# A message-passing layer whose scatter feeds nine epochs: the first group prepared alone, and the last filters made early

## The chip, the core and the metric

The kernel runs on one core of a Trainium2 chip. Its engines work side by side, each on its own list of instructions, in order, and wait for each other by semaphores: PE (TensorE, matmuls; PEld are its weight loads), DVE (VectorE), ACT (ScalarE), POOL (GpSimd) and SP (SyncE, which here only issues DMAs). The metric is the device time of one execution in microseconds (us), median of ten.

## What is computed

`x` has 12500 rows of 128; there are 400000 edges, sorted by `dst`, with `src` at random.

```python
h = jnp.maximum(_layernorm(x, axis=-1), 0.0)
h = h @ W_in2f.T                                           # then, with edge_attr as f_ij:
Wij = smu(f_ij @ W_f1.T + b_f1) @ W_f2.T + b_f2
Wij = Wij * edge_weight[:, None]
x_ij = h[dst] * Wij
agg = segment_sum(x_ij, src, num_segments=12500)
out = x + smu(agg @ W_o1.T + b_o1) @ W_o2.T + b_o2
```

Of every edge, a row of `h` (at `dst`) is multiplied by a filter `Wij`, made from its 20 attributes by two matmuls with a bent line (`smu`, an erf gate, done by a Gelu and a linear term) between them, and the product is summed into the row `src`.

## The kernel before

**Tiles.** An edge tile is 128 edges; 4 tiles are a *group* (512 edges, `GRP`), 8 tiles a *supertile* (`SUP`). There are 3125 tiles, 782 groups, 391 supertiles. The targets are cut in 98 *bins* of 128 rows.

**Epochs.** The supertiles are dealt to nine epochs (`PARTS`: 59, 59, 59, 59, 48, 37, 27, 27, 16). In its epoch, each tile's 128 messages go by one indirect DMA from POOL (`send`, L599) into a DRAM buffer of that epoch, `buf`, sorted by bin of `src`: each row to a slot that was counted for it. During the next epoch the buffer is read back (`fetch`, L630), and each bin is summed into `agg` by matmuls with a 0/1 matrix (`choose`, `se`, L641; `add`, `pg`, L654). One `add` matrix product of 128 rows is here called a *part*; an epoch has 98 bins times 6 parts (epochs 0 to 3), then 5, 4, 3, 3, 2. The last epoch's buffer is summed after the loop, with the two output matmuls interleaved.

**One pass of the loop** (`for g in range(NG)`) works on several groups at once, and its order is the program order of PE, DVE, ACT and SP, written by hand (`manual_schedule`); POOL and the DMAs follow by their waits:
- `turn(g)`, `send(g)`: PE transposes the messages (`pt`, L586), ACT copies them with the edge weight into `ms` (L596), POOL scatters (L599); `ms` has six buffers.
- `number(g+1)`, `weigh(g+1)` (second filter matmul, `pw`, L566), `gather(g+1)` (rows of `h` by a one-hot matmul on a window of 128 rows, `ph`, L547), `take(g+1)` (ACT copy, `hg`, L555), half of the parts of this pass, `mix(g+1)` (DVE product of filter and row, `mt`, L576).
- `hide(g+2)` (first filter matmul, `pu`, L516), `bend(g+2)` (Gelu, `ge`, L524), `count(g+2)` (`pc`, L464 and L465) and `read(g+2)` (four ACT reads, `jk`, L494), `smooth(g+2)` (DVE, `sm`, L532, reads `pu` and `ge`), `bins(g+3)`, the other half of the parts.
- three calls of `step()`, which in epoch 0 take the setup work off a list: the indices of the other tiles, the statistics and `h` of the other bins (24 units), the loads of `x`.

The parts of an epoch are spread evenly over its groups from the fifth on (`WAIT` = 4). PSUM has one bank each for `pu`, `pw`, `ph`, `pt`, `pc` (pool `ps1`, one buffer) and two for `pg`.

**The opening** (L682 to L722) loads the indices of 512 tiles, makes relative positions of `dst` (through a DRAM row `rel_dram` that is read back to all partitions, `rbc`), statistics and rows of `h` for the first four bins (`HEAD`), stores them in `h_dram` as three bfloat16 parts, reads windows of it back (`hw`), and takes groups 0 and 1 through the stages by hand. The stretch after the last scatter ("the end") is the last epoch's sum and the output.

The lines that set the parts' spread are

```python
lo = len(work) * (i - WAIT) // (ng - WAIT)
hi = len(work) * (i + 1 - WAIT) // (ng - WAIT)
```

Of the kernel before, what the change touches and what calls it, by code (L numbers as in the profile page):

```python
# [19 lines left out]
P = 128  # L20
# [14 lines left out]
BIG = 32768.0  # L35
ZP = 128


@with_exitstack
def gnn_kernel(  # L40
# [59 lines left out]
    bufs = [dram.tile([NB * CAP[k], ROW], F32, name=f"buf{k}") for k in range(EPOCHS)]  # L100
    tab = dram.tile([N + P, D], F32, name="tab")


# [157 lines left out]
    with tc.tile_pool(name="ld", bufs=4) as ld, \  # L261
# [13 lines left out]

        def fill(i):
            nc.vector.memset(fbufs[i], 1.0)

# [8 lines left out]
        def head_of(c):  # L287
# [5 lines left out]
            di, si, rel = rw[:, 0:n].bitcast(I32), rw[:, CH:CH + n].bitcast(I32), rw[:, 2 * CH:2 * CH + n]  # L293
            if c:
                rb = parts_tile()[:, :, 0, :]
            else:
                rb = edge.tile([P, SUP * P], BF, name="oh", bufs=3)[:, :CH].rearrange("p (j e) -> p j e", e=P)
            base_f = edge.tile([1, CH // SUP], F32, name="base_f")
# [7 lines left out]
            def based():  # L306
                nc.vector.tensor_copy(base_i[:, s0:s0 + m], di[0:1, 0:n:SUP])
                nc.vector.tensor_copy(base_f[:, :m], base_i[:, s0:s0 + m])
                nc.vector.tensor_copy(rel, di)

# [36 lines left out]
            def binned():  # L347
                nc.vector.tensor_scalar(di, si, 7, None, op0=ALU.arith_shift_right)
                nc.vector.tensor_copy(hi_b[:, a:a + n], di)

            def placed():
                nc.vector.tensor_scalar(di, si, P - 1, None, op0=ALU.bitwise_and)
                nc.vector.tensor_copy(lo_b[:, a:a + n], di)

            return dict(fetched=fetched, based=based, spread=spread, lowered=lowered, turned=turned, written=written,
                        limits=limits, bounded=bounded, binned=binned, placed=placed)


        one = head_of(0)
        one["fetched"]()  # L360
        nc.scalar.dma_start(x_sb[:, 0:HEAD, :], bin_rows(x, 0, HEAD))
        nc.scalar.dma_start(w_in, w_in_t)
        nc.vector.memset(w_f1, 0.0)
        nc.scalar.dma_start(w_f1[0:R, :], w_f1_t)
        nc.scalar.dma_start(w_f1[R:R + 1, :], b_f1)
        nc.scalar.dma_start(w_f2, w_f2_t)
        nc.scalar.dma_start(b2, b_f2.rearrange("o p -> p o"))
        nc.scalar.dma_start(w_sb[:, 0:CH], w_col[:, 0:CH])
        zr = edge.tile([P, 3 * D], BF, name="zr", bufs=1)
        nc.vector.memset(zr, 0.0)  # L370
        nc.scalar.dma_start(h_dram[NB * P:N + WIN, :], zr[:N + WIN - NB * P, :])
        for i in range(NF):
            fill(i)
        nc.vector.memset(zero, 0.0)
        clear(0, len(cleans) - 1, nc.scalar)
        spare = const.tile([P, 1], F32, name="spare")
        nc.scalar.activation(spare, eps, AF.Sqrt)

        def late_loads():

            nc.vector.memset(x_sb[:, NB - 1, :], 0.0)
            nc.vector.memset(w_sb[:, CH:CH + 1], 0.0)
            nc.gpsimd.dma_start(w_sb[:, CH:NT], w_col[:, CH:NT])
            nc.gpsimd.dma_start(w_o1, w_o1_t)
            nc.gpsimd.dma_start(w_o2, w_o2_t)
            nc.gpsimd.dma_start(b1, b_o1.rearrange("o p -> p o"))
            nc.gpsimd.dma_start(b2row, b_f2)
            nc.gpsimd.dma_start(bo2, b_o2.to_broadcast([P, P]))

# [7 lines left out]
        def load(s):  # L397
            if s >= NS:
                return
            t0, nt = sups[s]  # L400
            e0, n = t0 * P, nt * P
            fb = fbufs[s % NF]
            if s > 2:
                nc.sync.dma_start(fb[0:R, :n], f_t[:, e0:e0 + n])
            rb = ld.tile([P, SUP * P], BF, name="rbc")
            nc.sync.dma_start(rb[:, :n], rel_dram[:, e0:e0 + n].to_broadcast([P, n]))
            loaded[s] = (fb, rb)
            if s > 2:
                window(s)
# [18 lines left out]
        begins = {}  # L428

        def bins(g):  # L430

# [8 lines left out]
            if g in first:  # L440
                k = first[g]
                nc.vector.memset(co[:, 0], 0.0)
                m = sum(groups[i][1] for i in range(g, min(g + eps_of[k][1] * PER, NG)))
                begins[k] = (t, cnt.tile([P, max(n for _, n in eps_of) * SUP], F32, name="hic", bufs=2))
                nc.vector.tensor_scalar(begins[k][1][:, :m], hi_b[:, t:t + m], float(CAP[k]), None, op0=ALU.mult)
            else:
                pl, cl, nl = last.pop(0)
                nc.vector.tensor_add(co[:, 0], cl[:, nl - 1], pl[:, nl - 1])
# [60 lines left out]
        def hide(g):  # L509

            if g >= NG:
                return
# [6 lines left out]
        def bend(g):  # L519
            if g >= NG:  # L520
                return
            n = groups[g][1] * P
            ge = edge.tile([P, GRP * P], F32, name="ge")
            nc.scalar.activation(ge[:, :n], units_of[g][:, :n], AF.Gelu, scale=ZS)  # L524
            hidden[g] = ge

        def smooth(g):
            if g >= NG:
                return
# [20 lines left out]
        def take(g):  # L550
            if g >= NG:
                return
# [7 lines left out]
        def weigh(g):  # L560

            if g >= NG:
                return
            n = groups[g][1] * P
            pw = ps1.tile([P, GRP * P], F32, name="pw")
            nc.tensor.matmul(pw[:, :n], w_f2, hidden.pop(g)[:, :n], start=True, stop=True)  # L566
            pws[g] = pw

        mixed = {}

        def mix(g):
            if g >= NG:
                return
            n = groups[g][1] * P
            mt = edge.tile([P, GRP * P], F32, name="mt")
            nc.vector.scalar_tensor_tensor(mt[:, :n], pws.pop(g)[:, :n], b2, rows_of.pop(g)[:, :n],  # L576
                                           op0=ALU.add, op1=ALU.mult)
# [103 lines left out]
        WAIT = 4  # L681
        for s in range(3):  # L682
            nc.sync.dma_start(fbufs[s][0:R, :], f_t[:, s * SUP * P:(s + 1) * SUP * P])
        one["based"]()
        one["spread"]()
        one["bounded"]()
        one["lowered"]()
        one["turned"]()
        one["written"]()
        for s in range(3):  # L690
            load(s)
        nc.vector.tensor_scalar(w_f2, w_f2, GC, None, op0=ALU.mult)
        for b in range(HEAD):
            stats(edge, b)
        deviations(0, HEAD)
        rw = rowp.tile([P, ROWS, ROW], F32, name="rw")
        for step in rows_of_h(0, HEAD, *[rw[:, j * GRP:(j + 1) * GRP, 0:P] for j in range(3)], parts_tile(), bank):
            step()
        for s in range(3):
            window(s)  # L700
        late_loads()
        one["binned"]()
        bins(0)
        hide(0)
        bend(0)
        smooth(0)
        hide(1)
        bend(1)
        weigh(0)
        count(0)  # L710
        read(0)
        one["placed"]()
        pick(0)
        gather(0)
        number(0)
        take(0)
        mix(0)
        turn(0)
        send(0)
        smooth(1)  # L720
        bins(1)
        count(1)  # L722
        read(1)
        pick(1)
        bins(2)
        cleared = at_first = done = 0
        work = []
# [34 lines left out]
        single = [lambda b=b: stats(edge, b) for b in range(HEAD, NB)]  # L762
        steps = [one["limits"], loads.pop(0)]
        for c in range(1, NC):
# [4 lines left out]
            for f in mine:  # L769
                steps.append(f)  # L770
                if c > 1:
                    steps.append(single.pop(0))
        steps += loads
        for i in range(0, len(single), 2):
# [3 lines left out]
        for i in range(0, len(units_of_rows), 2):  # L778
            for pair in zip(*units_of_rows[i:i + 2]):
                steps += pair  # L780
        steps.append(output_bias)
        COUNT = len(steps)
        taken_steps = slot = 0

        def step():

            nonlocal taken_steps, slot
            slot += 1
            while taken_steps < COUNT and taken_steps * 3 * (eps_of[0][1] * PER - 12) < slot * COUNT:
                steps[taken_steps]()  # L790
                taken_steps += 1

        for g in range(NG):
            s = g // PER
            k = epoch[s]
            g0, ng = eps_of[k][0] * PER, min(eps_of[k][1] * PER, NG - eps_of[k][0] * PER)
            i = g - g0
            if g % PER == 0:
                load(s + 3)
# [21 lines left out]
            if k and i >= WAIT:  # L821
                lo = len(work) * (i - WAIT) // (ng - WAIT)
                hi = len(work) * (i + 1 - WAIT) // (ng - WAIT)
            if g:
                turn(g)
                send(g)
            step()
            number(g + 1)
            weigh(g + 1)
# [6 lines left out]
            bend(g + 2)  # L836
            count(g + 2)
            read(g + 2)
            smooth(g + 2)
            if g % PER == 0:  # L840
                pick((g + 4) // PER)
            bins(g + 3)
            parts(k - 1, hi)
            step()
            assert k == 0 or taken_steps == COUNT
# [225 lines left out]
```

## Time and profile before

| | |
|---|---|
| median of 10 runs | 4132.07 us (4129.55 to 4133.11) |
| the profiled execution | 4131.43 us, its span 4129.6 |
| PE busy | 3701.4 us (90%) |
| DVE, ACT, POOL busy | 3200.9, 2821.6, 3045.7 us |
| scatters (L599) | 3125, 0.963 us each |
| DMA | 834.71 MB, 202 GB/s over the span |
| first scatter, last scatter (start) | 32.90, 4020.17 us |

How to read it: busy time of an engine says little here, since the stages have different limits; POOL's issue time between two scatters does not count as busy. The trace lists instructions in order of time (start, duration, engine, line, operation, output and inputs, count, and in brackets the idle time ahead with what ended it); groups of instructions over a stretch (busy time, mean ns of one); and busy time stretch by stretch, with the count of instructions in brackets, then the granted clock of PE, the DMA engines' busy share and GB/s.

### The profile page before, as it was taken

What the parts mean: (1) busy time and instruction counts of PE and PEld (TensorE: products, weight loads), DVE (VectorE), ACT (ScalarE), POOL (GpSimd) and SP (SyncE); (2) the same over time, 40 slices, a digit from 0 to 9 for tenths busy, and PEclk for the clock granted to TensorE, in tenths of its full rate; (3) what the DMA queues carried; (4) which work ended last, traced back from release to release, by engine and by line L of the source; (5) the groups of instructions that cost most, each with busy time, mean ns of one, the idle gap of its engine ahead of it and who ended that gap; (6) DMA issues with size and microseconds to landing.
All of it is one profiled execution on the core that took longest, in us unless ns stands there. A gap on an engine that the chain in (4) does not pass through costs nothing. (4 is left out here: it accounts for less than half of the span.)

```text
span 4129.6 us, 74682 instructions
## 1 busy us (share of the span) xinstructions
PE 3701.4 (90%) x18498; PEld 2303.1 (56%) x18794; DVE 3200.9 (78%) x8553; ACT 2821.6 (68%) x11054; POOL 3045.7 (74%) x3165
## 2 busy tenths in 40 slices
PE   6878887999988999979999979999899899999999
PEld 2334434655545655546655546666566566565567
DVE  7888866877767877768877768888688788788777
ACT  5778875776666776657766757777677667677651
POOL 5777777777777777777777777777777777777762
PEclk9999998999999999989999989999999999999999
DMA  7857665766647666646666647676688689777568
GB/s 206 227 165 204 187 173 183 215 206 192 199 143 223 200 204 200 203 154 204 210 200 203 193 156 215 211 211 206 182 231 233 177 258 255 211 224 225 176 183 237
DMA packets 520970, 834.71 MB, mean 202 GB/s; under 512 B 84575, under 2 KB 334916, under 8 KB 520400
## 3 DMA queue, kind: packets, MB, share of 16 engines
q1 hardware_dynamic: 405932, 614.18, 51.8%
q0 software_dynamic: 100304, 208.14, 15.6%
q10 hardware_dynamic: 14292, 7.53, 0.6%
q8 instruction: 152, 2.49, 0.3%
q14 instruction: 290, 2.38, 0.2%
HBM read 456.16 MB, written 373.36 MB: 201 GB/s over the span
## 5 line engine op out<-in xcount | busy, mean ns | idle before, releaser
L599 POOL DMA_INDIRECT buf<-ms,ix x3125 | 3009.9, 963 | 990.0 <-issue 257.9
L654 PEld LDWEIGHTS pg<-se,rw 128*128 128x128 f32 x8036 | 1088.1, 192 | 152.0 <-issue 13.6
L596 ACT ACTIVATE ms<-pt,w_sb 128x128 f32<-128x128 f32 x3125 | 904.0, 392 | 358.7 <-DMA buf<-ms,ix 156.3
L654 PE MATMUL pg<-se,rw 128*128 128x128 f32 x8036 | 1109.6, 276 | 7.6 <-DVE se L641 7.6
L494 ACT ACTIVATE jk<-pc,nbig 128x98 f32<-128x98 f32 x3125 | 1025.9, 352 | 3.3 <-PE pc L465 2.7
L566 PE MATMUL pw<-sm,w_f 128*128 128x512 f32 x1564 | 882.1, 646 | 46.5 <-DVE sm L532 41.9
L524 ACT ACTIVATE ge<-pu 128x512 f32<-128x512 f32 x782 | 469.2, 600 | 550.3 <-PE pu L516 526.8
L576 DVE SCALAR_TENSOR_TENSOR mt<-pw,b,hg 128x512 f32<-128x512 f32 x782 | 583.7, 746 | 325.4 <-ACT hg L555 323.9
L516 PE MATMUL pu<-f,w_f 128*128 128x512 f32 x1564 | 809.8, 600 | 4.2 <-DVE sm L532 4.2
L586 PE MATMUL pt<-ident,mt 128*128 128x128 f32 x3125 | 495.5, 282 | 319.2 <-DVE mt L576 316.2
L641 DVE TENSOR_TENSOR se<-irow_ps,rw 128x1536 f32<-128x1536 f32 (+1 forms) x345 | 587.8, 1704 | 151.6 <-DMA rw<-buf 130.6
L532 DVE SCALAR_TENSOR_TENSOR sm<-pu,ge 128x512 f32<-128x512 f32 x782 | 536.0, 685 | 197.2 <-ACT ge L524 187.6
L494 ACT ACTIVATION_READ_ACCUMULATOR jk<-pc,nbig 128x1 f32 x3125 | 680.0, 218 | 0.0
L555 ACT ACTIVATE hg<-ph 128x512 f32<-128x512 f32 x782 | 470.0, 601 | 284.4 <-PE ph L547 282.4
L547 PE MATMUL ph<-oh,hw 128*128 128x512 bf16 x2050 | 626.1, 384 | 16.8 <-DMA hw<-h_dram 1.2
L586 PEld LDWEIGHTS pt<-ident,mt 128*128 128x128 f32 x3125 | 351.7, 142 | 416.0 <-DVE mt L576 408.3
L451 DVE TENSOR_TENSOR co<-co,po 128x98 f16<-128x98 f16 x2353 | 501.9, 213 | 81.2
L547 PEld LDWEIGHTS <-hw 128*128 128x128 bf16 x2346 | 231.7, 99 | 551.7 <-issue 451.1
L437 DVE TENSOR_TENSOR po<-irow_ps,hi_b 128x392 f16<-128x392 f32 x782 | 434.7, 556 | 0.0
L566 PEld LDWEIGHTS pw<-sm,w_f 128*128 128x128 f32 x1564 | 237.1, 191 | 176.3 <-DVE sm L532 172.6
L516 PEld LDWEIGHTS pu<-f,w_f 128*128 128x128 f32 x1564 | 251.8, 195 | 27.8 <-DVE sm L532 5.8
L464 PE MATMUL pc<-co,ones_h 128*128 128x392 f16 x782 | 258.6, 331 | 1.2 <-ACT ms L596 1.2
(119 smaller groups left out, 1699.5 us busy)
## 6 DMA issues: line engine op xcount, KB each, us to landing
rw<-buf SPq DMA_DIRECT2D x292, 774.0 KB
rbc<-rel_dram SPq DMA_DIRECT2D x390, 256.0 KB
buf<-zero SPq DMA_DIRECT2D x243, 387.0 KB
buf<-ms,ix POOLq DMA_INDIRECT x3125
buf<-zero SPq DMA_DIRECT2D x193, 258.0 KB
hw<-h_dram SPq DMA_DIRECT2D x391, 96.0 KB
rw<-buf SPq DMA_DIRECT2D x49, 645.0 KB
f<-in_f_t SPq DMA_DIRECT2D x390, 80.0 KB
```

Source lines behind the costliest of these rows:

```text
L451: nc.vector.tensor_add(co[:, j], co[:, j - 1], po[:, j - 1])
L494: nc.scalar.activation(jk, pc[:, j], AF.Relu, bias=nbig, accum_out=sl[:, j:j + 1])
L516: nc.tensor.matmul(pu[:, :n], w_f1, loaded[g // PER][0][:, o:o + n], start=True, stop=True)
L532: nc.vector.scalar_tensor_tensor(sm[:, :n], units_of.pop(g)[:, :n], LIN, hidden[g][:, :n], op0=ALU.mult, op1=ALU.add)
L547: nc.tensor.matmul(ph[:, :n], hw[:, q * D:(q + 1) * D], oh[:, o:o + n], start=(q == 0), stop=(q == 2))
L566: nc.tensor.matmul(pw[:, :n], w_f2, hidden.pop(g)[:, :n], start=True, stop=True)
L576: nc.vector.scalar_tensor_tensor(mt[:, :n], pws.pop(g)[:, :n], b2, rows_of.pop(g)[:, :n], op0=ALU.add, op1=ALU.mult)
L586: nc.tensor.transpose(pt[:, j, :], mt[:, j * P:(j + 1) * P], ident)
L596: nc.scalar.activation(ms[:, j, 0:P], pt[:, j], AF.Copy, scale=w_sb[:, t + j:t + j + 1])
L599: i = nc.gpsimd.indirect_dma_start(out=bufs[k][:, :], out_offset=bass.IndirectOffsetOnAxis(ap=ix[:, j:j + 1], axis=0), in_=ms[:, j, :], in ...
L641: nc.vector.tensor_tensor(se[:, :m], irow_ps.unsqueeze(1).to_broadcast([P, m, P]), rows_in[c][:, :m, P:P + 1].to_broadcast([P, m, P]), op= ...
L654: nc.tensor.matmul(pgs[0][:, g, :], rows_in[c][:, o, 0:P], sel[c][:, o, :], start=(q == 0), stop=(q == Q[k] - 1))
```

## The change

Two things are changed.

**The opening.** The first bin and the first 24 tiles (`FEW`, three supertiles) are prepared alone: their own small index loads (`ds`, `ss`), one bin's statistics and `h`, which stays in SBUF (`h_first`) and serves as the window of supertiles 0 to 2. Group 0 gets its one-hot from PE transposes (`spread_group`, `pick_group`). The rest of the first 512 tiles' preparation and bins 1 to 3 become a list `opening`, two items at each `step()` of the first passes. Fills and some loads go to POOL, six weight loads from POOL to steps on SP.

**The filters.** The filters of the last 43 supertiles (all of epochs 7 and 8, 86 groups) are made early: from group 126 on, at every fifth pass, `ahead_hide`, and in the next pass `ahead_smooth`, `ahead_weigh` and `ahead_keep`, make one group's filter, which SP stores in DRAM (`filters`). In the last 86 groups `hide`, `bend`, `smooth`, `take` and `weigh` return at once; `load` brings the filter (512 KB per supertile) in place of the attributes, and `mix` reads it from SBUF and the rows straight from `ph`. In the passes with early work the parts are thinned by 2.5 and 2.5, and the other passes take them.

```diff
+AHEAD_OF = 43
+EVERY = 5
...
+    SOON = NS - AHEAD_OF
+    filters = [dram.tile([P, SUP * P], F32, name=f"filter{s}") for s in range(SOON, NS)]
...
         one = head_of(0)
+        ds = edge.tile([P, FEW], I32, name="ds", bufs=1)
...
+        h_first = const.tile([P, 1, 3, D], BF, name="h_first")
+        nc.sync.dma_start(ds, dst_col[:, 0:FEW])
+        nc.scalar.dma_start(x_sb[:, 0:1, :], bin_rows(x, 0, 1))
+        nc.sync.dma_start(ss, src_col[:, 0:FEW])
+        nc.scalar.dma_start(w_in, w_in_t)
+        fill(0, nc.vector)
+        nc.gpsimd.memset(w_f1, 0.0)
+        nc.gpsimd.dma_start(w_f1[0:R, :], w_f1_t)
...
+        fill(1, nc.gpsimd)
+        nc.gpsimd.memset(zero, 0.0)
+        clear(0, len(cleans) - 1, nc.gpsimd)
+        fill(2, nc.gpsimd)
...
@@ def load(s)
-            if s > 2:
+            if s >= SOON:
+                nc.sync.dma_start(fb[:, :n], filters[s - SOON][:, :n])
+            elif s > 0:
                 nc.sync.dma_start(fb[0:R, :n], f_t[:, e0:e0 + n])
...
@@ hide, bend, smooth, take, weigh
-            if g >= NG:
+            if g >= NG or g // PER >= SOON:
                 return
...
+        ahead = [g for g in range(NG) if g // PER >= SOON]
+        ahead_of = {}
+        for i, g in enumerate(ahead):
+            ahead_of[eps_of[0][1] * PER + 8 + i * EVERY] = g
...
+        def ahead_hide(g):
...
+            pu = ps1.tile([P, GRP * P], F32, name="pu")
+            nc.tensor.matmul(pu[:, :n], w_f1, fx[:, o:o + n], start=True, stop=True)
+            ge = edge.tile([P, GRP * P], F32, name="ge")
+            nc.scalar.activation(ge[:, :n], pu[:, :n], AF.Gelu, scale=ZS)
+            if g + 1 < NG and (g + 1) % PER == 0:
+                ahead_load(g + 1)
...
+        def ahead_smooth(g):
...
+            nc.vector.scalar_tensor_tensor(sm[:, :n], units_of.pop(g)[:, :n], LIN, hidden[g][:, :n],
+                                           op0=ALU.mult, op1=ALU.add)
...
+        def ahead_weigh(g):
...
+            pw = ps1.tile([P, GRP * P], F32, name="pw")
+            nc.tensor.matmul(pw[:, :n], w_f2, hidden.pop(g)[:, :n], start=True, stop=True)
...
+        def ahead_keep(g):
...
+            wx = edge.tile([P, GRP * P], F32, name="ge")
+            nc.scalar.activation(wx[:, :n], pws.pop(g)[:, :n], AF.Copy)
+            nc.sync.dma_start(filters[g // PER - SOON][:, o:o + n], wx[:, :n])
...
@@ def mix(g)
+            if g // PER >= SOON:
+                o = g % PER * GRP * P
+                pws[g] = loaded[g // PER][0][:, o:o + n]
...
@@ the opening, in order
+        nc.vector.tensor_copy(dsf, ds)
+        pb0 = spread_group(0)
...
+        stats(edge, 0)
+        few = edge.tile([FEW, P], BF, name="few", bufs=1)
+        nc.scalar.activation(few, pd[:FEW, 0:P], AF.Copy)
+        nc.sync.dma_start(rel_dram[0, 0:FEW * P].rearrange("(t e) -> t e", e=P), few)
+        few_bins()
+        deviations(0, 1)
...
+        normed()
+        turned()
...
+        pick_group(0, pb0)
+        shorn()
...
+        hide(0)
...
+        for b in range(1, HEAD):
+            stats(edge, b)
+        deviations(1, HEAD)
+        nc.scalar.activation(spare[:, 1:2], eps, AF.Gelu)
+        product()
+        bins(0)
...
+        first_part()
         bend(0)
+        other_parts()
         smooth(0)
+        pb1 = spread_group(1)
         count(0)
         read(0)
         gather(0)
         number(0)
         take(0)
+        weigh(0)
         mix(0)
...
         turn(0)
         send(0)
+        hide(1)
...
+        opening = [one["based"], heads[0], one["spread"], heads[1], one["lowered"], heads[2], one["turned"], heads[3],
+                   one["written"], heads[4], one["bounded"], heads[5], one["binned"], other_starts]
...
@@ the loop
-                lo = len(work) * (i - WAIT) // (ng - WAIT)
-                hi = len(work) * (i + 1 - WAIT) // (ng - WAIT)
+                load_of = [2.5 * (g0 + j in ahead_of) + 2.5 * (g0 + j - 1 in ahead_of) for j in range(WAIT, ng)]
+                even = (len(work) + sum(load_of)) / (ng - WAIT)
+
+                def upto_group(j):
+                    return len(work) if j == ng else min(len(work), max(0, round(even * (j - WAIT) - sum(load_of[:j - WAIT]))))
+                lo, hi = upto_group(i), upto_group(i + 1)
             if g:
                 turn(g)
                 send(g)
             step()
+            if g - 1 in ahead_of:
+                ahead_smooth(ahead_of[g - 1])
             number(g + 1)
             weigh(g + 1)
             gather(g + 1)
             take(g + 1)
             parts(k - 1, lo + (hi - lo) // 2)
             mix(g + 1)
             step()
             hide(g + 2)
             bend(g + 2)
             count(g + 2)
+            if g - 1 in ahead_of:
+                ahead_weigh(ahead_of[g - 1])
             read(g + 2)
+            if g - 1 in ahead_of:
+                ahead_keep(ahead_of[g - 1])
             smooth(g + 2)
             if g % PER == 0:
                 pick((g + 4) // PER)
             bins(g + 3)
             parts(k - 1, hi)
+            if g in ahead_of:
+                ahead_hide(ahead_of[g])
             step()
```

## The prediction

> **What bounds the kernel now.** I read the page first, then POOL's scatter line and the message copies that feed it over chosen stretches, then one group of the loop in order of time. The page:
>
> ```profile
> span 4129.6 us, 74682 instructions
> ...
> L599 POOL DMA_INDIRECT buf<-ms,ix x3125 | 3009.9, 963 | 990.0 <-issue 257.9
> ```
>
> Its first part gives POOL 74% of the span, PE 90%. POOL looks idle for a quarter, but its 3125 scatters are spaced by 0.96 us of work and about 0.30 us of issue. The second view, stretch by stretch, has L599 alone (stretch, length, busy, count):
>
> ```profile
> 700.00:860.00 160.00, 121.57 (x127) 1.00 0.68 208
> ...
> 2480.00:2880.00 400.00, 303.63 (x317) 1.00 0.71 213
> ...
> 3850.00:4000.00 150.00, 104.08 (x109) 0.97 0.70 211
> ```
>
> 127 scatters in 160 us is 1.26 us each, 5.05 us per group of four; nearly every stretch has that rate. Scatters start at 32.9, the last at 4020.2. So the span is 32.9 (opening) + 3124 x 1.263 = 3945.6 + 41.7 (lost between scatters) + 109.4 (the end after the last scatter). By the scatters' starts, epoch 0 loses 13.7 of the 41.7 (608.6 us for 471 intervals), epoch 8 loses 13.5 (170.1 for 124). **POOL sets the end, wherever the other engines supply a group in under 5.05 us.** How near they are, the same view of L596, the message copies (four per group), shows:
>
> ```profile
> 700.00:860.00 160.00, 39.29 (x136) 1.00 0.68 208
> ...
> 2480.00:2880.00 400.00, 93.59 (x324) 1.00 0.71 213
> ```
>
> In 700-860 the supply made 34 groups, 4.71 us each, and ran ahead of POOL; in epoch 4, 81 groups in 400 us, 4.94 each. Slack: 0.34 us per group in epochs 1 to 3, 0.11 in epoch 4. One group of that stretch, in order of time (start, duration):
>
> ```profile
> 786.51 1.03 PE L516 MATMUL pu<-f,w_f 128*128 128x512 f32 x2
> ...
> 787.37 0.33 PE L464 MATMUL pc<-co,ones_h 128*128 128x392 f16 x1
> ...
> 787.57 0.60 ACT L524 ACTIVATE ge<-pu 128x512 f32<-128x512 f32 x1 [0.71 <-PE pu L516]
> 787.70 0.83 PE L654 MATMUL pg<-se,rw 128*128 128x128 f32 x6
> ...
> 788.20 0.69 DVE L532 SCALAR_TENSOR_TENSOR sm<-pu,ge 128x512 f32<-128x512 f32 x1 [0.55 <-ACT ge L524]
> ...
> 788.37 0.60 PE L586 MATMUL pt<-ident,mt 128*128 128x128 f32 x4
> ```
>
> PE goes from step to step without a hole: from start to start `pu` takes 0.86, the counts 0.33, two matmuls of the add (one part) 0.22; in the lines ahead of these `pw` began at 784.46, the gather `ph` at 785.42, the next add at 786.07, so 0.96 and 0.65. PE sets the supply. And `sm`, which frees the only `pu` bank, ends at 788.89, after `pt` has begun.
>
> **The change, the opening.** Before, the first mix starts at 30.50 and the first scatter comes 2.4 us later:
>
> ```profile
> 30.50 0.75 DVE L576 SCALAR_TENSOR_TENSOR mt<-pw,b,hg 128x512 f32<-128x512 f32 x1 [1.10 <-ACT hg L555]
> ...
> 32.90 1.03 POOL L599 DMA_INDIRECT buf<-ms,ix  x1 [11.64 <-ACT ms L596]
> ```
>
> The new chain, by rows of before's first 33 us: indices land 2.0 us after issue at 0.75 (a store of `rel` issued at 12.61 frees its reload at 14.61), DVE is busy with a 0.91 fill until 3.2; five transposes to 4.8 (four took 1.16); ACT `few` and the first deviation to 5.4; reciprocal and normalising to 5.95; transpose and relu to 6.8; PE's `pu` (1.92) and the product to 8.5. ACT meanwhile waits for three more bins' statistics (8.1), a deviation, the Gelu table (1.28) and a dummy, to 9.9; two casts, a Gelu (0.60) and two DVE subtractions to 11.4; gather 1.5, copy 0.6, `pw`, to 14.6; mix to 15.4; first scatter 1.6 later, 17.0. POOL's new work there (fills of 0.91 to 1.6 each by the DVE fill and POOL's own 0.20 for an eighth; five DMAs of 0.6; clears) is over by 13. Gain 15.9. Then group 1: PE has a spread, three transposes and the adjoining steps ahead of its `turn`, where the second group trails by 9.7 us already now (32.90 to 42.63); I take 3 us off and bound the gain by 8 and 18. **-13.**
>
> The rows price these matmuls at a half-speed rate (1.92 for `pu`, 1.03 later) although the granted clock reads 0.97. The Trainium skill ("TensorE: Matmul & The Clock Gate", section "Part 1: The HAM clock gate") says that the array runs at half clock until about 3.4 us of sustained activity. By it `pw` and the gather would be warm already and the first scatter come near 15.4, an estimate; before's rows show 1.9 us pairs as late as 34 us, and I go by those.
>
> Six weight loads move from POOL to SP (0.4 us of issue each, in steps of epoch 0 that nobody awaits soon): nothing.
>
> **The end.** The last 86 groups lose `pu`, `pw`, Gelu, copy and `sm`: 1.82 us of PE, 1.2 of ACT, 0.69 of DVE each. In epoch 8 PE needs 5.4 to 5.6 per group; 3.7 is below POOL's 5.05, so its 13.5 go, and some 1.9 of epoch 7's. The reads grow from 80 to 512 KB per 10.1 us, 44 GB/s more on stretches with 219 to 226 and a busy share of 0.74 to 0.79; they are issued three supertiles (30 us) ahead, and the 774 KB fetches of rows land within 6 us. Should the queues fill up, late rows cost 0 to 6. **-15.** The 109 us after the last scatter are untouched.
>
> **The same work, early.** 86 groups move to groups 126 to 551, one in five: 22, 24, 24 items in epochs 1 to 3, 16 in epoch 4. The parts of the add are only shifted (5 fewer in the item's two groups, more elsewhere). An item costs PE 0.86 + 0.96 = 1.82, plus its waits:
> - `ahead_hide` needs the bank `pu`, which `smooth(g+2)` has just been given to read. PE arrives 0.86 + 0.33 + 2 x 0.22 = 1.64 after `pu`'s start; `sm` ends 2.38 after it (786.51 to 788.89). Wait 0.75. Behind it on PE stands everything else, first the `turn` of the next messages, for which ACT and POOL wait.
> - `ahead_keep` stands on ACT behind four reads (788.07 to 789.33, 2.82 after `pu`) and ends at 3.42; the next `pw` wants its bank at 0.86 + 0.33 + 0.96 + 0.44 + 0.58 = 3.17. Wait 0.25 to 0.3; the next message copies, behind the copy on ACT, need `turn` and come later anyway.
> - 25 of the 86 items have a choice (`se`, 1.75 on DVE) beside `ahead_smooth`: 0.3 to 0.8 each, 0.15 on average.
>
> Together 3.0 us. Against that, PE idles a little today (4.3 us before `pt` over the 34 groups, 0.63 per five); as fewer late mixes are met I take 0.5 back. **An item costs 2.5 of supply, the slack of five groups is 1.7.** So 0.8 x 70 = 56, less the lead that each epoch starts with (POOL's lag is 4 to 8 us there and 2 to 3 where it starves: 5 + 2 + 2): 47. Epoch 4: 16 x (2.5 - 0.55) - 2 = 29. **+76.** Bounds per item: 1.2 (no wait, all idle time refilled) to 3.3 (nothing absorbed, more collisions). The store of each filter (256 KB per 25 us, 10 GB/s) waits on SP for ACT; behind it are fetches of rows issued four tiles ahead, and the load of the next early group, which waits for PE, has four groups' time: nothing.
>
> Sum against the profiled execution, 4131.4 (span 4129.6 and 1.8 around it, 0.6 below the median): 4131.4 - 13 - 15 + 76 = **4180**.
>
> **Rivals.** (1) *Hidden, faster*: no bank waits, PE refills its idle time, an item costs 1.2: epochs 1 to 3 lose nothing, epoch 4 16 x 0.65 - 2 = 8; 4131 - 28 + 8 = 4111. It decides below about 1.95 us per item, where the losses equal 28. For it: ACT and DVE have 25% and 18% free. Against: the 0.75 comes from three rows. (2) *Overrun*: nothing is absorbed, 3.0 to 3.3 per item: 70 x 1.3 to 1.6 - 9, and 16 x 2.45 to 2.75 - 2: 119 to 145; 4222 to 4248. (3) *The opening doesn't do what it is made for*, since group 1 waits as long as group 0 gained: 13 more, 4193.
>
> **Chances.** Forecast (with 3 inside it, 4145 to 4215) 0.62; overrun 0.12; hidden 0.18; near balance 0.08. A measurement of this kernel tells about 0.2% (8 us) from no change. Range 4115 to 4220: it takes in most of the hidden case and the edge of the overrun. Faster 0.18, same 0.08, slower 0.74.
>
> **What will show it.** First scatter at 15 to 20 us; L599 below 79 per 100 us from 750 to 2850, worst in epoch 4, and 79 again in the last three epochs; PE waiting before the early `pu` for DVE `sm`, 0.7 us in the mean, and before `pw` for ACT. I am wrong if the counts stay at 79 through epochs 1 to 3 while `pt` follows the early `pu` without a wait on `sm`.

## The result, and the profile after

The changed kernel takes 4207.26 us (median of 8 runs, 4199.87 to 4212.41), the kernel before 4131.48 (28 runs): ratio 1.0181, 95% interval 1.0172 to 1.019. It is slower by 76 us, inside the range and 27 above the forecast. The profiled execution has a span of 4202.8. From the page of the kernel after, its span, the engines' shares of the chain that ended last, and the scatters (busy, mean ns, idle before):

```profile
span 4202.8 us, 74541 instructions
...
PE 49%; DVE 15%; DMA 10%; ACT 6%; issue 4%; POOL 1%; DVEq 0%; SPq 0%; ACTq 0%; POOLq 0%
...
L681 POOL DMA_INDIRECT buf<-ms,ix x3125 | 3010.6, 963 | 1074.4 <-issue 309.1
```

A scatter still takes 963 ns. POOL only idles more, 1074 us in place of 990, and PE holds half of the chain. Where the time went is read from the scatters' starts, epoch by epoch (us; the last column is the last scatter's start):

| kernel | first scatter | epoch 1 begins | epochs 1 to 4 | epochs 5 to 7 | epoch 8 | last |
|---|---|---|---|---|---|---|
| before | 32.9 | 642.8 | 2282.8 | 924.5 | 170.1 | 4020.2 |
| after | 19.2 | 646.4 | 2366.0 | 924.4 | 156.8 | 4093.6 |
| after less before | -13.7 | +3.6 | +83.2 | -0.1 | -13.3 | +73.4 |

Of the 83.2, epochs 1, 2 and 3 lose 19.2, 20.0 and 19.5, epoch 4 loses 24.6. The opening's 13.7 are all given back before epoch 1: group 1's first scatter is still 12.4 us ahead of before's (30.2 for 42.6) and group 4's 6.4, but group 5's is 2.3 behind. The scatters over three of the stretches that the prediction showed (stretch, length, busy and count, clock, DMA share, GB/s), and over one each that lies nearly all in epochs 5 and 6:

```profile
700.00:860.00 160.00, 117.87 (x123) 1.00 0.67 201
2480.00:2880.00 400.00, 290.92 (x302) 1.00 0.69 206
3020.00:3395.00 375.00, 284.70 (x297) 0.97 0.77 219
3400.00:3680.00 280.00, 210.79 (x221) 0.98 0.86 246
3850.00:4000.00 150.00, 113.81 (x119) 0.85 0.72 230
```

127 became 123 and 317 became 302: 76.9 and 75.5 per 100 us in epochs 1 and 4, and 79 again from epoch 5 on. The last stretch had 109 in epoch 8 before; its 119 now are of the end of epoch 7 and the start of epoch 8, which begins at 3936.8. The message copies that feed them (L678) now have no more in store:

```profile
700.00:860.00 160.00, 34.62 (x120) 1.00 0.67 201
2480.00:2880.00 400.00, 86.46 (x300) 1.00 0.69 206
```

Before, 136 copies stood against 127 scatters; now 120 against 123. POOL takes what it is given.

**Why PE gives less.** PE's groups between 700 and 2900 us, busy and idle before them. First the kernel before, the transposes:

```profile
L586 PE MATMUL pt<-ident,mt 128*128 128x128 f32 x1744 | 274.2, 280 | 175.4 <-DVE mt L576 173.6
```

Then the kernel after:

```profile
L601 PE MATMUL pw<-sm,w_f 128*128 128x512 f32 x836 | 458.7, 631 | 18.5 <-ACT ge L645 14.3 <-DVE sm L567 1.6
L551 PE MATMUL pu<-f,w_f 128*128 128x512 f32 x838 | 430.3, 595 | 7.1 <-DVE sm L631 6.6
...
L668 PE MATMUL pt<-ident,mt 128*128 128x128 f32 x1672 | 256.0, 276 | 32.8 <-DVE mt L658 32.3
...
L621 PE MATMUL pu<-fx,w_f 128*128 128x512 f32 x168 | 94.6, 645 | 69.8 <-DVE sm L567 69.8
L638 PE MATMUL pw<-sm,w_f 128*128 128x512 f32 x166 | 92.0, 636 | 9.2 <-DVE mt L658 8.3
```

Before, PE stood 175.4 us ahead of the transposes: that was its slack, 0.40 us in the mean of the 436 groups of 5.05 us. After, 32.8 are left. In its place PE waits 69.8 ahead of 84 early products, 0.83 each, for the `smooth` that still reads the bank, and 14.3 ahead of `pw` for ACT's early copy. One such place, in order of time:

```profile
791.34 0.69 DVE L567 SCALAR_TENSOR_TENSOR sm<-pu,ge 128x512 f32<-128x512 f32 x1 [0.55 <-ACT ge L559]
...
792.09 1.12 PE L621 MATMUL pu<-fx,w_f 128*128 128x512 f32 x2 [0.64 <-DVE sm L567]
793.05 0.60 PE L668 MATMUL pt<-ident,mt 128*128 128x128 f32 x4
793.49 1.02 PE L601 MATMUL pw<-sm,w_f 128*128 128x512 f32 x2
```

The last two rows show how idle time is counted: the transposes count as busy until 793.65, yet `pw` starts at 793.49. The end of a matmul is modelled, and a wait that lies under it does not appear as idle time. The idle times above are therefore too small; from start to start the waits can be had in full, and two experiments need that.

**The opening.** DVE and POOL of the kernel after, while the first group is made:

```profile
3.67 5.31 DVE L765 TENSOR_SCALAR ds<-ss 128x24 int32<-128x24 int32 x1
...
4.61 0.97 POOL L281 MEMSET f<- 128x1024 f32 x1
...
7.98 0.97 POOL L281 MEMSET f<- 128x1024 f32 x1
...
9.23 0.18 DVE L767 TENSOR_SCALAR ds<-ss 128x24 int32<-128x24 int32 x1
...
17.07 0.75 DVE L658 SCALAR_TENSOR_TENSOR mt<-pw,b,hg 128x512 f32<-128x512 f32 x1 [0.69 <-PE pw L601]
...
19.22 1.07 POOL L681 DMA_INDIRECT buf<-ms,ix  x1 [9.59 <-ACT ms L678]
```

L765 and L767 are alike in shape; the one took 5.31 us and ended with POOL's last fill (8.95), the other 0.18. After the first scatter POOL starves again: holes (time beyond the usual 1.26 from scatter to scatter) of 5.8, 4.5, 1.6, 8.7 and 4.3 us ahead of the scatters at 30.2, 39.7, 46.5, 65.3 and 74.7, 25 in all, where before had one of 4.6 at 42.6. Two of their causes, on PE ahead of group 2's `pw`, and on SP and DVE ahead of group 5:

```profile
29.52 1.04 PE L329 MATMUL pg<-ident,rw 128*128 128x128 f32 x4 [3.06 <-DVE ix L538]
...
30.35 1.48 PE L209 MATMUL pg<-w_in,rw 128*128 128x128 f32 x6
...
31.63 1.71 PE L601 MATMUL pw<-sm,w_f 128*128 128x512 f32 x2
```

```profile
44.13 2.14 SPq L872 DMA_DIRECT2D agg<-in_x  x2
46.31 4.98 SPq L307 DMA_DIRECT2D rw<-in_dst_col  x1
...
56.28 0.20 DVE L311 COPY base_i<-rw 1x64 int32<-1x64 int32 x1 [6.61 <-DMA rw<-in_dst_col]
```

Two items of the opening's list (L329, L209) hold PE for 2.1 us after a wait of 3.06. And the indices of the next 512 tiles are issued behind two pieces of `x` (768 KB each): the issue alone took 4.98, and DVE, with everything behind that copy, waited 6.61.

### The profile page after: what moved, and what is told of

The parts are those of the page before. It is cut to its first block, busy times and chain, and to the rows that moved or that the text cites. A ratio compares the mean times of both kernels' runs of the same rounds, so it can differ in the third digit from the quotient of the medians.

```text
span 4202.8 us, 74541 instructions
## 1 busy us (share of the span) xinstructions
PE 3698.0 (88%) x18493; PEld 2321.2 (55%) x18803; DVE 3215.5 (77%) x8557; ACT 2834.7 (67%) x11060; POOL 3050.9 (73%) x3173
## 4 chain that ended last, share of the span: by engine, by line
PE 49%; DVE 15%; DMA 10%; ACT 6%; issue 4%; POOL 1%; DVEq 0%; SPq 0%; ACTq 0%; POOLq 0%
PE pg L736 12%; PE pw L601 11%; DMA buf<-ms,ix 9%; PE pu L551 8%; PE ph L582 7%; DVE se L723 5%; PE pt L668 5%; DVE mt L658 3%; DVE sm L567 2%; ACT jk L529 2%; ACT ge L559 2%; PE pu L621 2%; DVE agg L749 1%; DVE co L486 1%; PE pc L499 1%
## 5 line engine op out<-in xcount | busy, mean ns | idle before, releaser
L736 PEld LDWEIGHTS pg<-se,rw 128*128 128x128 f32 x8036 | 1099.3, 193 | 208.3 <-issue 75.8
L678 ACT ACTIVATE ms<-pt,w_sb 128x128 f32<-128x128 f32 x3125 | 904.1, 391 | 262.3 <-PE pt L668 128.6
L601 PE MATMUL pw<-sm,w_f 128*128 128x512 f32 x1392 | 769.7, 635 | 58.2 <-DVE sm L567 37.3
L559 ACT ACTIVATE ge<-pu 128x512 f32<-128x512 f32 x696 | 417.3, 600 | 555.8 <-PE pu L551 541.8
L658 DVE SCALAR_TENSOR_TENSOR mt<-pw,b,hg 128x512 f32<-128x512 f32 x696 | 520.0, 747 | 329.8 <-ACT hg L590 323.2
L551 PE MATMUL pu<-f,w_f 128*128 128x512 f32 x1392 | 721.4, 600 | 7.1 <-DVE sm L631 6.6
L567 DVE SCALAR_TENSOR_TENSOR sm<-pu,ge 128x512 f32<-128x512 f32 x696 | 478.2, 687 | 252.5 <-ACT ge L559 242.8
L582 PE MATMUL ph<-oh,hw 128*128 128x512 bf16 (+1 forms) x2019 | 614.8, 386 | 16.7 <-issue 0.7
L590 ACT ACTIVATE hg<-ph 128x512 f32<-128x512 f32 x696 | 418.0, 601 | 305.9 <-PE ph L582 305.0
L486 DVE TENSOR_TENSOR co<-co,po 128x98 f16<-128x98 f16 x2353 | 501.9, 213 | 81.2
L601 PEld LDWEIGHTS pw<-sm,w_f 128*128 128x128 f32 x1392 | 209.8, 190 | 152.4 <-DVE sm L567 115.9
L500 PE MATMUL pc<-po,tri 128*128 128x392 f16 x782 | 259.9, 332 | 0.0
```

Of the source, the lines that this page charges most:

```text
L486: nc.vector.tensor_add(co[:, j], co[:, j - 1], po[:, j - 1])
L551: nc.tensor.matmul(pu[:, :n], w_f1, loaded[g // PER][0][:, o:o + n], start=True, stop=True)
L567: nc.vector.scalar_tensor_tensor(sm[:, :n], units_of.pop(g)[:, :n], LIN, hidden[g][:, :n], op0=ALU.mult, op1=ALU.add)
L582: nc.tensor.matmul(ph[:, :n], hw[:, q * D:(q + 1) * D], oh[:, o:o + n], start=(q == 0), stop=(q == 2))
L678: nc.scalar.activation(ms[:, j, 0:P], pt[:, j], AF.Copy, scale=w_sb[:, t + j:t + j + 1])
L736: nc.tensor.matmul(pgs[0][:, g, :], rows_in[c][:, o, 0:P], sel[c][:, o, :], start=(q == 0), stop=(q == Q[k] - 1))
```

## The experiments

Each is compared with runs of the kernel before on the same chip and of the same time, since these differ: its medians were 4131 to 4147 us beside the result and e1 to e8, and 5212 and 5224 beside e9 to e12. Ratios carry their 95% interval; microseconds by a ratio are of 4131. Unless a diff says otherwise, the base is the changed kernel.

**e1, e2: one part alone.** For e1 `AHEAD_OF = 0` and the two steps for `fx` are left out; e2 is the kernel before with all of the early filters.

> The changed opening alone, no filters made early. Theory (the parts are independent, as the scatters' starts have it: the first scatter came 13.7 us sooner, but epoch 0 ended 3.7 us later): 4131.5 + 3.7 = 4135. Rival (the opening did gain its 13 us, and the early work's own steps in epoch 0 took them): 4131.5 - 13 = 4118.

> The kernel before with the early filters alone (43 supertiles, one group in five), its opening untouched. Theory: epochs 1 to 4 lose what they lost in the changed kernel, 83.2 us, and epoch 8 gains 13.4: 4131.5 + 69.8 = 4201. Rival (part of the 83 comes from the new opening, whose late start leaves epoch 1 without a lead): under 4190.

e1: 1.0015 (1.0006 to 1.0025), +6 us. First scatter 19.1; epochs 1 to 4 2283.4, epoch 8 171.9, as before. e2: 1.0186 (1.0168 to 1.0205), +77 by the ratio; epochs 1 to 4 2369.6, epoch 8 157.2. The parts add up within the intervals: the early filters make the whole loss, and the opening gains nothing by itself. Its rival explanation, that the early work's steps took its gain, falls. A single trace tells the opening's worth to some 5 us only: epoch 1 begins at 646.4 in the changed kernel and at 653.7, 644.6, 644.2 and 649.5 in e1, e3, e4 and e5, which have the same opening; with the old one at 642.8, and at 648.9 and 648.6 in e2 and e8.

**e3: the early product later,** behind the next pass's `send`; its `smooth` behind the next `mix`.

```diff
+            if g - 1 in ahead_of:
+                ahead_hide(ahead_of[g - 1])
             step()
-            if g - 1 in ahead_of:
-                ahead_smooth(ahead_of[g - 1])
...
             mix(g + 1)
+            if g - 1 in ahead_of:
+                ahead_smooth(ahead_of[g - 1])
...
-            if g in ahead_of:
-                ahead_hide(ahead_of[g])
```

> The changed kernel with the early product of w_f1 moved behind the next pass's turn and send, and its smooth step moved behind the next mix, so that the product no longer meets a pu bank that smooth is still reading. Theory (the bank wait is 0.75 of an item's 2.5 us of supply): epochs 1 to 3 give back 0.75 x 70 = 52 us, epoch 4 0.75 x 16 = 12; 4207 - 64 = 4143. Rival (PE's own 1.82 us of products is the whole price, and the wait only moves to the next product that wants the bank): 4200 to 4207.

1.0485 (1.0468 to 1.0503), +200: worse than either theory. PE's groups over the same stretch of e3:

```profile
L551 PE MATMUL pu<-f,w_f 128*128 128x512 f32 x790 | 417.4, 610 | 143.4 <-DVE sm L631 143.4
...
L621 PE MATMUL pu<-fx,w_f 128*128 128x512 f32 x158 | 88.9, 645 | 9.3 <-DVE sm L567 8.3 <-issue 0.6
```

The early product waits no more (9.3), but the regular `pu` of the same pass now finds the bank held by the early `smooth`, which I had put behind the mix: 143.4 us over 79 items, 1.8 each. The wait moved and doubled, and the time followed: from start to start, over epochs 1 to 4, the step to the regular `pu` takes 161 us longer than in the changed kernel and all the others 26 less, 135 in all.

**e4: the early copy ahead of the reads.**

```diff
+            if g - 1 in ahead_of:
+                ahead_keep(ahead_of[g - 1])
             read(g + 2)
-            if g - 1 in ahead_of:
-                ahead_keep(ahead_of[g - 1])
```

> The changed kernel with the early filter's copy out of the pw bank put ahead of the four reads of counts on ACT. Theory (PE's next product waits 0.25 to 0.3 us for that bank in each item): 86 x 0.28 = 24 us less, 4183. Rival (PE comes later than the copy anyway, the wait is covered): 4207.

1.012 (1.0103 to 1.0137): 25 us back, as the theory had it. The wait of `pw` for ACT is gone, that for the `pu` bank is where it was:

```profile
L601 PE MATMUL pw<-sm,w_f 128*128 128x512 f32 x845 | 461.6, 628 | 2.8 <-DVE sm L567 1.5 <-ACT ge L645 0.8
...
L621 PE MATMUL pu<-fx,w_f 128*128 128x512 f32 (+1 forms) x170 | 96.0, 647 | 71.7 <-DVE sm L567 71.7
```

The wait shows as 14.3 us, 0.17 each, while epochs 1 to 4 are 26 shorter. The rest is the part that lies under the transposes' modelled end: over epochs 1 to 4 the time from the start of the transposes to the start of `pw` adds up to 262.5 us in the changed kernel and to 234.6 here, 28 less, 0.32 for each of the 86 items. So theory and size are both right.

**e5: another bank** (e4 with the early product in the bank of the gather).

```diff
-            pu = ps1.tile([P, GRP * P], F32, name="pu")
+            pu = ps1.tile([P, GRP * P], F32, name="ph")
```

> The kernel of e4 (the early copy ahead of the reads) with one word more: the early product of w_f1 takes the bank ph, free at that place, in the place of the bank pu that smooth is still reading. Theory (the 0.84 us that PE stood before each early product, 71.7 us over 85 items in e4, is lost supply): 4185 - 64 to 72 = 4113 to 4121, and e3's 132 us came only from the next product's wait for the same bank. Rival (PE's 1.82 us of products is the price, and the gather now waits for ph as the others did for pu): 4175 or more.

1.0164 (1.0147 to 1.0181): no gain, 18 us lost against e4. The lines of e5 over the same stretch:

```profile
L582 PE MATMUL ph<-oh,hw 128*128 128x512 bf16 x1086 | 328.3, 380 | 104.1 <-DVE sm L631 95.0 <-issue 0.2
...
L621 PE MATMUL ph<-fx,w_f 128*128 128x512 f32 x168 | 86.1, 594 | 0.0
```

The early product starts at once, and the next gather waits 95.0 us, 1.13 per item, for the early `smooth`, which stands on DVE behind `bins`, and in some passes behind a choice. From start to start, over epochs 1 to 4, `pw` to the gather takes 111.5 us longer than in e4, and the steps that lead up to the two `pu` products 94 less: 17 of the 18 us. The rival's second half was right.

**e6: POOL's fills away from the first group.** POOL's order is not written by hand. In the program, `fill(1)` to `fill(3)` and `zr` were put behind `send(0)`, with the loads that need them, and `zero` ahead of the weight loads.

> The changed kernel with POOL's fills of f(1) to f(3) and zr put behind the first four scatters and the fill of zero ahead of the weight loads, so that POOL fills nothing between 2.5 and 14 us. Theory (the 5.31 us of the shift ds<-ss on DVE, which ended with POOL's last fill at 8.95, are DVE held up by POOL's fills): the shift takes under 0.5, the first scatter comes at 14 to 15; of the total 0 to 5 us come back, since groups 1 to 6 wait for other things. Rival (the indices ss landed late, at 9): the shift ends near 9 all the same and the first scatter is at 19.

The edit did not do that: POOL ran the fills at 5.8 to 8.9 all the same. Yet it tells the theories apart:

```profile
4.35 0.14 DVE L758 TENSOR_SCALAR ds<-ss 128x24 int32<-128x24 int32 x1
...
5.45 3.50 DVE L760 TENSOR_SCALAR ds<-ss 128x24 int32<-128x24 int32 x1
...
5.80 1.86 POOL L281 MEMSET f<- 128x1024 f32 x2
...
7.94 0.97 POOL L281 MEMSET f<- 128x1024 f32 x1
```

The shift (L758, L765 in the changed kernel), free of fills this time, takes 0.14, so its indices had landed; the next instruction of its shape, which meets the fills, takes 3.50 and ends with the last. Total 1.0188 (1.0171 to 1.0205), as the changed kernel.

**e7: chunk 1's indices first.**

```diff
-        steps = [one["placed"], loads.pop(0), one["limits"]]
+        steps = [one["placed"]]
...
+            if c == 1:
+                steps += [mine.pop(0), loads.pop(0), one["limits"]]
             if loads:
                 steps.append(loads.pop(0))
```

> The changed kernel with the two index loads of chunk 1 issued ahead of the first two pieces of x (768 KB each) on SP. Theory (DVE's 6.6 us before the cast of chunk 1's indices made the 8.8 us hole before the scatters at 65.3): that hole shrinks to 1 to 3 us and the end comes 5 to 8 us sooner, 4200. Rival (PE's order and its clock make the hole): 8 us stay, 4207.

Before the hole's scatter, first in the changed kernel, then the same scatter in e7, with the issue of the indices and DVE's copy, which waits no more:

```profile
65.34 0.96 POOL L681 DMA_INDIRECT buf<-ms,ix  x1 [9.05 <-issue]
```

```profile
42.35 0.47 SPq L307 DMA_DIRECT2D rw<-in_dst_col  x1
...
47.99 0.39 DVE L311 COPY base_i<-rw 1x64 int32<-1x64 int32 x1
...
55.55 0.96 POOL L681 DMA_INDIRECT buf<-ms,ix  x1 [0.72 <-issue]
```

The hole of 8.7 us is 0.4 and the one after it 3.0 in place of 4.3, but two new ones (1.1 and 1.8) follow. Epoch 1 begins at 640.4, 6.0 sooner than in the changed kernel and 2.4 sooner than before, and sooner than in any other trace. Total 1.0163 (1.0146 to 1.018), 7 us less by the ratios, though the intervals meet: the hole's cause is shown, the gain in the total is not.

**e8: fewer items, further apart.** The kernel before with early filters, `AHEAD_OF = 16`, `EVERY = 12`.

> The kernel before, its opening untouched, with the filters of epoch 8 alone (16 supertiles, 32 groups) made early, one group in twelve. Theory (twelve groups of epochs 1 to 3 have 12 x 0.34 = 4.1 us of slack for an item's 2.5 to 3): nothing is lost there and epoch 8's 13.4 are gained: 4131.5 - 13.4 = 4118, ratio 0.9968. Rival (POOL runs with so little ahead that each item stalls it at once and slack beside it doesn't help): 32 x 1.5 = 48 lost, 4166.

0.9974 (0.9964 to 0.9984), 11 us faster. Epochs 1 to 4 take 2283.1, as before, and epoch 8 157.0. PE's lines of e8, the transposes and the early product:

```profile
L638 PE MATMUL pt<-ident,mt 128*128 128x128 f32 x1744 | 270.2, 278 | 81.2 <-DVE mt L628 79.5
...
L591 PE MATMUL pu<-fx,w_f 128*128 128x512 f32 (+1 forms) x62 | 35.2, 650 | 37.8 <-DVE sm L538 37.8
```

An item waits longer for its bank than in the changed kernel (37.8 us over 31, 1.22 each) and costs nothing: it is paid from the idle time ahead of the transposes, 175.4 before and 81.2 here, 3.0 us for each of the 31.

**e9 and e11: no bank wait left?** e4 with the early product in `ph`, its Gelu ahead of the reads and its `smooth` in the same pass:

```diff
-            if g - 1 in ahead_of:
-                ahead_smooth(ahead_of[g - 1])
...
             count(g + 2)
+            if g in ahead_of:
+                ahead_hide(ahead_of[g])
...
             smooth(g + 2)
+            if g in ahead_of:
+                ahead_smooth(ahead_of[g])
...
-            if g in ahead_of:
-                ahead_hide(ahead_of[g])
```

> The kernel of e4 with the early product in the bank ph, its Gelu ahead of the four reads on ACT and its smooth step in the same pass, right behind smooth(g+2), so that the bank is free again before the next gather wants it. In e5 the gather waited 1.13 us per item for that smooth step (95.0 us over 84 items) where e4 had waited 0.84 before the early product (71.7 us). Theory (the price of an item beyond PE's 1.82 us of products is PE's waiting for banks, wherever it falls): PE's waits around an item fall below 0.3 us and the time to 4113 to 4125, ratio 0.996 to 0.999. Rival (the waits on PE are cover for something that is late anyway, ACT or DVE, and taking them away gives nothing): 4185 or more, ratio 1.012 and up.

> The kernel of e9 once more, since e9 ran on a chip whose granted clock was 0.895 (the kernel before took 5212 us there, and PE set the pace everywhere), so that it said nothing of the price of an item at 0.97. Theory (an item's price beyond PE's products is PE's waiting for banks): PE's waits before L621, L582, L601 and L638 sum to under 25 us in epochs 1 to 4, and the ratio is 0.996 to 0.999. Rival (the waits cover what is late anyway): ratio 1.012 as in e4, or more.

Both ran where PE was granted a lower clock, as e10 and e12 did: e9 and e10 on chip 10, e11 and e12 on chip 15, which had granted e1 to e4 0.97. The span and the clock of e11 (0.903 in e12):

```profile
core 0: 5266.4 us, clock 0.902
```

The kernel before takes 5212 and 5224 us there. e9: 1.0088 (1.0051 to 1.0126), e11: 1.0076 (1.0048 to 1.0103), outside the theory's bounds. PE's waits ahead of the four products, which were to stay under 25 us, are 426 us in e11 from 700 to 3500 us: the early product now waits for the copy that reads the gather's bank, and for 180 of the 426 the profile shows no cause. A scatter comes only every 1.6 to 1.7 us in the mean of the loop, so POOL no longer sets the end, and the price of an item at 0.97 is not measured by them. **Whether early work without bank waits would be free stays open.**

**e10: DVE does the fills** (e1 with e7's edit, and each POOL fill given to DVE between the first group's steps).

> The changed opening alone (as e1) with POOL's fills given to DVE, between the steps of the first group, and the index loads of chunk 1 issued early as in e7. In e6 POOL had run its fills at 5.8 to 8.9 all the same, and another small DVE instruction (the mask ds<-ss of bins' low parts, 3.50 us) ended with the last of them, while the shift took 0.14. Theory (a DVE instruction that starts beside POOL's fills ends with them): no DVE instruction of the first 15 us takes over 1.1, the first scatter comes at 14 to 16, epoch 0 ends 2 to 5 us before e7's 639; total 4125 to 4130, ratio 0.998 to 0.9995. Rival (groups 1 and 2 wait for the steps put ahead of them on PE, whenever group 0 comes): first scatter 15, but epoch 0 ends at 638 to 640, ratio 1.000.

Its total, 0.9947 (0.9904 to 0.999), belongs to those slower conditions; its first 20 us ran at a granted clock of 1.00 and can be read:

```profile
3.67 0.14 DVE L755 TENSOR_SCALAR ds<-ss 128x24 int32<-128x24 int32 x1
...
4.10 0.18 DVE L757 TENSOR_SCALAR ds<-ss 128x24 int32<-128x24 int32 x1
...
13.24 1.86 PE L593 MATMUL pw<-sm,w_f 128*128 128x512 f32 x2
...
17.38 1.03 POOL L671 DMA_INDIRECT buf<-ms,ix  x1 [11.23 <-ACT ms L668]
```

No small DVE instruction is held up. The first scatter comes at 17.4 and not at 14 to 16, since two fills of 0.91 now stand in DVE's own chain and `pw` takes 1.86 where the changed kernel's took 1.15. Group 1 follows at 29.2 (30.2 in the changed kernel) after a hole of 6.5: the 1.8 us shrink to 1.0 within one group, as the rival had it. The clock granted from 20 to 40 us was 0.91 in both.

**e12: the parts that helped, together:** `AHEAD_OF = 16`, `EVERY = 12`, e4's and e7's edits.

> The changed kernel with 16 supertiles early in the place of 43 (epoch 8 alone), one group in twelve, the early copy ahead of the reads (e4) and chunk 1's index loads first (e7). Theory (the parts add up: e8's 10.8 us of gain, and an opening whose epoch 0 ends 2 us sooner than before's in e7): 4131.5 - 11 - 2 = 4118, ratio 0.9965, bounds 0.995 to 0.998. Rival (the opening of e7 costs something that its 43 filters hid, as e1's 6 us had it): ratio 0.998 to 1.000.

0.9946 (0.9916 to 0.9976) at the low clock: it beats the kernel before there. At 0.97 it was not run; what is shown there is e8's 0.9974.

## Why the prediction was right, and where it was wrong

**The bound and the direction: right.** POOL sets the end where it is fed in 5.05 us, PE sets the supply, and an item's 2.5 us exceeds the slack of five groups. The counts fell and recovered where the text said. e8 shows it from the other side: 32 such items, one in every twelfth group, with 12 x 0.40 = 4.8 us of slack for each, cost nothing. The thinning of the parts and the stores of the filters, which no run tries alone, are in e8 too.

**The price of an item: right in the main.** From start to start the two early products take PE 0.96 and 0.95 in the mean (forecast 0.86 and 0.96, 1.82 together). As idle time the wait for `pu` was 0.83 (0.75), that for ACT's copy 0.17 (0.25 to 0.3; 0.32 in full, by e4), the regular `pu` and the early `pw` wait 0.08 and 0.10: 3.1 us together, 3.0 in the forecast. Against 5 x 0.40 = 2.0 of slack that would be 1.1 in each of 86 items, 95 us against 83 measured. PE's idle time ahead of the transposes, over epochs 1 to 4 of the kernel before, then of the changed kernel:

```profile
L586 PE MATMUL pt<-ident,mt 128*128 128x128 f32 x1800 | 283.5, 280 | 198.9 <-DVE mt L576 197.0
```

```profile
L668 PE MATMUL pt<-ident,mt 128*128 128x128 f32 x1800 | 276.1, 276 | 56.5 <-DVE mt L658 56.0
```

142.4 us of it were used and 83.2 of time lost: 2.6 for each of the 86 items (forecast 2.5), 3.0 in e8. So the account is good to some 0.4 us an item, and not better; not all of the slack is used. That a wait for the bank is lost supply is shown by e3 and e5: the wait moved, and the time followed it.

**Epochs 1 to 3: 47 forecast, 58.6 measured.** The failed term is "less the lead that each epoch starts with", 9 us. Each of the three lost the same 19 to 20, which is 0.8 x 23.3 = 18.7 with no lead taken off. The trace shows no lead to take. In the changed kernel a message waits 25.2 us from its copy's end to its scatter at the start of epoch 1 (mean of eight), but 5.8 in that epoch's groups 6 and 7, just ahead of the first item, and 4.2 and 6.4 at the starts of epochs 2 and 3; over these epochs the mean is 4.6 to 4.9. So the level of starving is near 5, not 2 to 3, and the lead above it was about 1 us. Epoch 4: 29 forecast, 24.6 measured.

**The opening: wrong, and the largest miss.** The failed step is "Gain 15.9. Then group 1 ... I take 3 us off", -13; measured +3.6 in the changed kernel's trace and +6 in e1. The number of rival 3, which I had kept inside the forecast's chance, is what came; its reason is not. Group 1 kept 12.4 us of the 13.7, and groups 2 to 6 spent them: 8.1 were left at group 2, 6.4 at group 4, and at group 6 the new kernel was 6.6 behind. Two things were mis-sized:
- "POOL's new work there ... is over by 13", taken as costless. It held DVE: L765 took 5.31 for 0.14, and the first scatter came at 19.2 in place of 17.0. e6 and e10 show it. The Trainium skill ("SBUF — State Buffer", section "SBUF: two separate sides") says that VectorE, in its 2-port modes or with two inputs in SBUF against a GpSimd instruction that reads SBUF, and GpSimd lock one pair of ports against each other: whichever starts first has it for the whole instruction, and the other stands still. The traces of the changed kernel and of e6 agree in that DVE ended with POOL's last fill, and e10's in that nothing is held up without fills; that DVE waited across several of POOL's instructions, 5.31 us, is more than the rule says, and no run shows in which mode L765 works.
- The work taken out of the first group's way was not gone, but on a list, two items at each step, ahead of groups 1 to 6 on PE, DVE and SP. I priced its first place only (3 us); five holes cost 25. e7 took out one, 8.7 to 0.4.

On the matmuls' speed the rule of the clock gate (the page and section that the prediction names) had the better price: in the changed kernel `pw` at 15.81 took 1.15, where I had put a row of 1.92. It had it for that product alone: in e10 the same product, at 13.24, after pauses of PE of 1.29 and 0.41 us in the steps ahead of it, took 1.86, and group 2's, at 31.63, took 1.71.

**The end: right.** Epoch 8 gained 13.3 (13.5 forecast). Epoch 7 gained nothing, not 1.9: it ran at POOL's pace before as after. The longer reads cost nothing that the scatters show.

Sum: the miss of 27 us is 16 to 17 from the opening, 11.6 from epochs 1 to 3 (9 of it the lead) and 1.6 from the end, less 4.4 in epoch 4, and 2.6 between the profiled run and the median. The range was meant to take in most of the hidden case, but its lower end, 4115, lies above that case's own 4111.

## What to carry to other kernels

Work that is moved to a stage with spare time is free as long as its price, waits for buffers included, is below the slack between two such items; price the slack in the limiting stage's own idle time and space the items by it (one in twelve, for 16 supertiles, gained 11 us; one in five, for 43, lost 77). A single-buffered bank has a chain of its own (product, Gelu, `smooth`): in each of the orders tried at 0.97 a second user made somebody wait, and moving an instruction only chose who. Taking work off the first item's path gains only what the next items do not wait for: follow the list up to where the old order is caught up.

## What the runs showed of the hardware that was not expected

A small DVE instruction (128x24, 0.14 to 0.18 us alone) that met POOL's fills took 5.31 and 3.50 us and ended with the last fill. Both began ahead of the first fill by the trace (3.67 for 4.61, 5.45 for 5.80); what held them so early is not shown. In e6 two more DVE instructions, beside POOL's fill of `zero` at 1.67, took 1.08 and 1.07 where they take 0.40 and 0.39 in the changed kernel. POOL's issues of DMAs held DVE up less: in e10 four such instructions took 0.14 to 0.30 us while POOL issued two loads, but in e6 a cast beside them took 0.89 (0.21 in e10).

In e9 to e12 PE was granted 0.90 of its clock in the mean, 0.97 in e1 to e8, and the kernel before took 26% longer. That is not the chip as such, since chip 15 shows both. DVE, ACT and POOL worked as fast per instruction (a scatter 966 ns in e12, 962 in e8, from 700 to 3500 us); longer are waits for which the profile shows no cause (180 us ahead of DVE's `smooth` in e12, 2.3 in e8). Whether the low clock caused them or came of them is open.
